# First attention of a two-part transformer kernel: key maximum added by the tensor engine, copies and small steps moved between engines

## The chip, the cores and the metric

The kernel runs on one core of one Trainium2 chip. The metric is device time in microseconds (us). A core has five engines that run at the same time, each with its own queue of instructions in order: PE (matrix multiplies; its weight loads are listed as PEld), DVE (vector work), ACT (activation functions and copies), POOL (general vector work, in SBUF only) and SP, which issues the DMAs. Matmul results stand in PSUM, eight banks of 512 f32 columns for 128 partitions; everything else stands in SBUF.

## The reference, cut to what matters

Sixteen sequences of 256 positions with 128 channels pass through a first windowed attention, then through six layers of attention and feed-forward. The change touches the first attention only:

```
x = x + first(layernorm(x))
# first: 64 windows of 64 positions, 16 heads of 8 channels
qkv = (xw @ W_qkv).reshape(B * nw, 64, 3, 16, 8)
q = layernorm(q, ln_gamma, ln_beta)      # over the 8 channels of a head
k = layernorm(k, ln_gamma, ln_beta)
attn = softmax(einsum('bqhd,bkhd->bhqk', q * SCALE, k))   # SCALE = 1
out = einsum('bhqk,bkhd->bqhd', attn, v).reshape(B * nw, 64, 128)
out = out @ W_proj + b_proj
...
x = x + six_layers(layernorm(x))         # attention + feed-forward, not touched
```

## The kernel before

**The two parts.** `first_attention` (lines 297 to 547) runs first, in PSUM pools and SBUF pools of its own. When its pools are given back, the main loop (from line 906) runs 192 tiles of the six layers; there the order of PE is pinned by hand. In the first attention it is not: the compiler is called with a scheduling option (line 1015) and orders each engine's instructions from its own estimates of their times, so the order on an engine is not that of the program text. What each engine gets is in order from then on: an instruction that waits holds all that stand behind it in its queue.

**Units and stages.** The first attention works on eight units of two sequences: four token tiles (t) of 128 positions, each of which holds two windows (c). The outer loop has 25 steps k; in each, `merge` interleaves pieces of six stages that belong to different units, so that several units are in flight:

- `stage_load`: `row_stats` gets the mean and the sum of squares of each row (lines 319 to 323) on ACT, the weight of the values `rv` on DVE (370); PE transposes the tile, ACT and DVE write it as two halves, `xnt`; POOL adds the projection's bias to `xt` (378), for later.
- `stage_qkv`: three matmuls per token tile into a bank `pq` (387); ACT and DVE write q and k (388) and the values as fp16 high and low halves (392, 393). Then, for all 32 heads of q and k, squares (ACT, 397), their sums (DVE, 399), `rsqrt` on 128 columns (DVE and ACT in turn, 307 to 313), the scaling (DVE, 401), gamma and beta (POOL, 402 and 403).
- `stage_heads`: q (s = 0) and k (s = 1) are written as fp16 halves with four places per head: the high half by ACT (414), the low half by POOL (415), and the second copies of both by DVE (417, 419). A transposing DMA on SP's queue turns them (421).
- `stage_soft`: sixteen small matmuls fill one bank `ps` (439; two banks, `bufs` 2), DVE takes the maximum over keys (448) and subtracts it on the way to SBUF (449). When a token tile is whole, ACT takes the exponential (459) and writes the high half (461), POOL the low half (462), and a transposing DMA turns both (464).
- `stage_out`: per window half c, 24 matmuls with the values into a bank `po` (480), DVE takes the reciprocal of the sums (482) and multiplies (485); then a PE transpose (493), an ACT copy (495), the projection (500) and the sum with x (DVE, 507).
- `stage_norm`: the result goes out by DMA (513), `row_stats` again, scaled rows on ACT (518), PE transposes (522) and two ACT copies into `xg` (524, 525), from which the main loop starts.

**Weights.** From step 6 on the first layer's weights are loaded and prepared in between (`first_weights`), which takes some ACT, DVE and PE time.

**PSUM.** `SPLIT0` (line 34) gives the banks of the first attention: two for `pq`, two for `ps`, two for `po`, one for `py`, one for `pt`.

Of the kernel before, what the change touches and what calls it, by code (L numbers as in the profile page):

```python
# [12 lines left out]
HP = mybir.dt.float16  # L13
# [20 lines left out]
SPLIT0 = (2, 2, 2, 1, 1)  # L34
# [21 lines left out]
def kernel(  # L56
# [30 lines left out]
    make_identity(nc, ident)  # L87
    onesm = const.tile([128, 128], F32, name="onesm")
# [208 lines left out]
    def first_attention(p1, p2, p3, pqp, psp0, pop, pyp, ptp=None):  # L297
        ptp = ptp or pyp
        def rsqrt(dst, src, scale):
            if dst.shape[1] != 128:  # L300
                S.activation(dst, src, AF.Ln, bias=epst, scale=scale)
                S.activation(dst, dst, AF.Exp, scale=-0.5)
                return
            n = dst.shape[1]
            a = p3.tile([128, n], F32, name=f"rqa{n}")
            b = p3.tile([128, n], F32, name=f"rqb{n}")
            V.tensor_scalar(b, src, scale, EPS, ALU.mult, ALU.add)
            S.activation(a, b, AF.Ln)
            S.activation(a, a, AF.Exp, scale=-0.5)
            V.tensor_tensor(b, b, a, ALU.mult)  # L310
            V.tensor_tensor(b, b, a, ALU.mult)
            V.tensor_scalar(b, b, -0.5, 1.5, ALU.mult, ALU.add)
            V.tensor_tensor(dst, b, a, ALU.mult)

        def row_stats(xt, pre):
            mu = p3.tile([128, 4], F32, name=f"{pre}mu")
            rs = p3.tile([128, 4], F32, name=f"{pre}rs")
            sq = p3.tile([128, 128], F32, name="sq0")
            for t in range(4):
                S.activation(sq, xt[:, t], AF.Copy, scale=-1.0 / 128.0, accum_out=mu[:, t : t + 1])  # L320
            for t in range(4):
                S.activation(sq, xt[:, t], AF.Square, bias=mu[:, t : t + 1], accum_out=rs[:, t : t + 1])
            rsqrt(rs, rs, 1.0 / 128.0)
            return mu, rs
# [22 lines left out]
        dma(bpt, bp0.partition_broadcast(128))  # L347
        pm = pqp.tile([128, 512], F32, name="pq")
# [15 lines left out]
        def stage_load(u):  # L364
            if u:
                load_x(u)
            e = U[u]
            _, e.rs = row_stats(e.xt, "a")
            e.rv = p1.tile([128, 4], F32, name="rv")
            V.tensor_scalar(e.rv, e.rs, VPRE, None, ALU.mult)  # L370
            yield
            e.xnt = p1.tile([128, 2, 4, 128], FR, name="xnt")
            pt = ptp.tile([128, 4, 128], F32, name="pt" if ptp is not pyp else "py")
            for t in range(4):
                T.transpose(pt[:, t], e.xt[:, t], ident)
            S.copy(e.xnt[:, 0], pt)
            V.tensor_tensor(e.xnt[:, 1], pt, e.xnt[:, 0].bitcast(F32), ALU.subtract)
            G.tensor_tensor(e.xt, e.xt, bpt.unsqueeze(1).to_broadcast([128, 4, 128]), ALU.add)
            yield
# [26 lines left out]
        def stage_heads(u):  # L406
            e = U[u]
            e.hl = []
            for s in range(2):
                src = e.qk[:, :, s * 128 : s * 128 + 128].rearrange("p t (h d) -> p t h d", d=8)  # L410
                hl = p1.tile([128, 4, 16, 4, 8], HP, name=f"hl{s}")
                for t in range(4):
                    hi, lo = hl[:, t, :, 0], hl[:, t, :, 2 if s else 1]
                    S.copy(hi, src[:, t])
                    G.tensor_tensor(lo, src[:, t], hi, ALU.subtract)
                    if s:
                        V.tensor_copy(hl[:, t, :, 1:4:2], hl[:, t, :, 0:3:2])
                    else:
                        V.tensor_copy(hl[:, t, :, 2:4], hl[:, t, :, 0:2])
# [7 lines left out]
        def stage_soft(u, n2):  # L427
            e = U[u]
            p0 = p2.tile([128, 2, 8, 128], F32, name="p0")
            for n in range(2):  # L430
                t = 2 * n2 + n
                for jj in range(2):
                    ps = psp0.tile([128, 4, 2, 64], F32, name="ps")
                    for i in range(4):
                        for c in range(2):
                            cols = slice(64 * c, 64 * c + 64)
                            for vp in range(2):
# [5 lines left out]
                                    start=True,  # L443
                                    stop=True,
                                )
                    nm = p2.tile([128, 8], F32, name="nm0", bufs=4)
                    psf = ps.rearrange("p i c k -> p (i c) k")
                    V.tensor_reduce(nm, psf, AX.X, ALU.max)
                    V.tensor_tensor(
                        p0[:, n, 4 * jj : 4 * jj + 4].rearrange("p i (c k) -> p (i c) k", c=2),  # L450
                        psf,
                        nm.unsqueeze(2).to_broadcast([128, 8, 64]),
                        ALU.subtract,
# [3 lines left out]
            for n in range(2):  # L457
                pf = p0[:, n]
                S.activation(pf, pf, AF.Exp)
                ph = p2.tile([128, 2, 8, 128], HP, name="ph")  # L460
                S.copy(ph[:, 0], pf)
# [5 lines left out]
        def stage_out(u, n2):  # L467
            e = U[u]
            for n in range(2):
# [3 lines left out]
                o0 = p3.tile([128, 2, 8, 8], F32, name="o0")  # L473
                for c in range(2):
                    r = slice(64 * c, 64 * c + 64)
                    po = pop.tile([128, 8, 18], F32, name="po")
                    for gm in range(8):
                        p = gm % 4 * 2 + gm // 4
                        for q, (a, b) in enumerate(((0, 0), (0, 1), (1, 0))):
                            T.matmul(po[:, p], pt0[r, a * 8 + gm], v[r, b, p], start=(q == 0), stop=(q == 2))  # L480
                    rc = p3.tile([128, 8], F32, name="rc0")
                    V.reciprocal(rc, po[:, :, 16])
                    for hp in range(2):
                        h = slice(64 * hp, 64 * hp + 64)
                        V.tensor_tensor(
                            o0[h, c],
                            po[h, :, hp * 8 : hp * 8 + 8],
                            rc[h].unsqueeze(2).to_broadcast([64, 8, 8]),
                            ALU.mult,
                        )  # L490
# [76 lines left out]
    identh = keep.tile([128, 128], HP, name="identh")  # L567
    V.tensor_copy(identh, ident)
# [451 lines left out]
```

## Time and profile before

| | us |
|---|---|
| median of 3 runs (lowest, highest) | 3285.94 (3284.38, 3286.59) |
| profiled execution, its own time | 3280.49 |
| its span, first to last instruction | 3278.7 |
| granted PE clock, mean | 0.996 |

The span cut into stretches, busy us of each engine:

| stretch, us | PE | DVE | ACT | POOL |
|---|---|---|---|---|
| 0 to 50 | 19.39 | 31.66 | 34.22 | 21.41 |
| 260 to 290 | 22.26 | 20.28 | 19.56 | 20.01 |
| 290 to 3278 | 2851.68 | 2359.46 | 2176.59 | 2347.06 |

The first stretch is the start of the first attention; its first score matmul (L439) begins near 52 us, its last one ends near 254.7. In 260 to 290 the last units leave while the main loop begins: its first matmul starts at 269.72, and the last copy into `xg` ends at 286.7. From there on the main loop runs alone.

How to read it: busy time is the time an engine had an instruction in work. The duration of a matmul includes the time to pass through the array, so matmuls in a row overlap and cost less than the mean of one. A row of the groups gives line, engine, operation, output and inputs, shapes, count, then busy us and mean ns of one, then the idle time of the engine just before such instructions, with what ended it.

### The profile page before, as it was taken

Reading aid. Unit: us, or ns where it says so; the run is one execution under the profiler, and the core shown is the slowest. Engines: PE = TensorE matmul, PEld = TensorE weight load, DVE = VectorE, ACT = ScalarE, POOL = GpSimd, SP = SyncE. Lnnn points to the kernel's source line nnn. Section 1 sums busy time; section 2 is a strip of 40 time slices with the busy share of each in tenths; the row PEclk is TensorE's granted clock in tenths of the full one; section 3 lists DMA queues with packets and bytes.
Section 4 is the critical chain, followed back from the end, with each engine's and each line's share of the span. In section 5 each row is a group of like instructions: output and inputs, shape, how many; then the busy total and the mean of one; then the engine's idle time right before and its main releaser. Section 6 shows DMA issues by size and latency. Waiting matters only on the chain. (4 is left out here: it accounts for less than half of the span.)

```text
span 3278.7 us, 159366 instructions
## 1 busy us (share of the span) xinstructions
PE 3062.1 (93%) x70178; PEld 2157.8 (66%) x70178; DVE 2596.0 (79%) x4850; ACT 2388.8 (73%) x5034; POOL 2511.2 (77%) x2578
## 2 busy tenths in 40 slices
PE   4887999999999999999999999999999999999996
PEld 3665666666666666666666666666666666666664
DVE  7987788887788887788787788887788887777773
ACT  6876777777777777777777777777777777766773
POOL 5657888877888877888877888878888778777771
PEclk9999999999999999999999999999999999999998
DMA  4763444344354343454343344444454443434442
GB/s 110 132 130 77 99 101 102 83 88 91 82 104 99 83 90 88 83 107 95 84 92 85 86 108 92 85 95 82 89 104 91 91 90 81 91 89 90 86 88 56
DMA packets 622969, 303.31 MB, mean 93 GB/s; under 512 B 533446, under 2 KB 545732, under 8 KB 622276
## 3 DMA queue, kind: packets, MB, share of 16 engines
q1 hardware_dynamic: 622276, 293.11, 42.7%
q8 instruction: 552, 9.04, 1.1%
q14 instruction: 141, 1.16, 0.1%
HBM read 22.38 MB, written 4.19 MB: 8 GB/s over the span
## 5 line engine op out<-in xcount | busy, mean ns | idle before, releaser
L291 PE MATMUL bank<-wqkv,xhl 128*128 128x512 f16 x3456 | 1238.3, 380 | 7.9 <-ACT sq L651 7.6
L653 POOL TENSOR_TENSOR sum<-mc 128x512 f32<-128x512 f32 x768 | 993.9, 1297 | 285.7 <-DVE mc L642 275.0
L642 DVE TENSOR_TENSOR mc<-bank,tq 128x1024 f32<-128x1024 f32 x768 | 929.8, 1220 | 186.1 <-PE bank L294 178.3
L663 POOL TENSOR_TENSOR sum<-sum,r 128x512 f32<-128x512 f32 x768 | 797.6, 1059 | 31.9
L652 DVE TENSOR_REDUCE r<-sq 128x8 f32<-128x512 f32 x768 | 519.8, 682 | 283.2 <-ACT sq L651 276.0
L294 PE MATMUL bank<-ident,sum 128*128 128x128 f32 x3072 | 712.9, 273 | 24.2 <-DVE of L796 24.2
L801 POOL TENSOR_TENSOR ohl<-of,ohl 128x512 f16<-128x512 f32 x384 | 451.3, 1175 | 226.0 <-ACT ohl L800 225.3
L651 ACT ACTIVATE sq<-bank 128x512 f32<-128x512 f32 x768 | 458.7, 608 | 150.6 <-DVE mc L642 148.3
L294 PEld LDWEIGHTS bank<-ident,sum 128*128 128x128 f32 x3072 | 432.4, 141 | 182.2 <-issue 67.6
L291 PEld LDWEIGHTS <-xhl 128*128 128x128 f16 x3456 | 340.0, 98 | 181.8 <-issue 17.9
L800 ACT CAST ohl<-of 128x512 f16<-128x512 f32 x384 | 237.8, 619 | 283.9 <-DVE of L796 278.9
L291 PE MATMUL bank<-vb,pt 64*32 64x65 f32 x6144 | 384.5, 225 | 31.6 <-ACT pt L620 21.0
L291 PEld LDWEIGHTS bank<-vb,pt 64*32 64x32 f32 x6144 | 263.0, 105 | 191.5 <-ACT p L275 49.0
L294 PE MATMUL bank<-ident,p 128*128 128x128 f32 x1536 | 354.8, 273 | 0.9 <-issue 0.9
L291 PEld LDWEIGHTS bank<-kt,qt 64*32 64x32 f32 x27648 | 289.1, 105 | 91.6 <-issue 91.6
L291 PE MATMUL bank<-v,pt 64*32 64x65 f32 x6144 | 319.5, 225 | 30.1 <-ACT gt L281 13.4
L291 PE MATMUL bank<-vw,pt 64*32 64x65 f32 x12288 | 336.5, 225 | 0.0
L291 PE MATMUL bank<-kt,qt 64*32 64x64 f32 (+1 forms) x27648 | 312.9, 216 | 9.5 <-issue 9.5
L291 PE MATMUL bank<-ot,wohl 128*128 128x128 f16 x4608 | 294.8, 221 | 4.6 <-DMA ot<-ohl 4.6
L796 DVE TENSOR_TENSOR of<-bank,rc 128x256 f32<-128x256 f32 x768 | 292.4, 416 | 1.6
L620 ACT COPY kt<-bank 128x512 f32<-128x512 f32 x384 | 226.3, 589 | 70.9 <-PE bank L294 65.1
L291 PEld LDWEIGHTS <-wohl 128*128 128x128 f16 x4608 | 261.8, 99 | 22.7 <-DMA ot<-ohl 4.8
(155 smaller groups left out, 5130.5 us busy)
## 6 DMA issues: line engine op xcount, KB each, us to landing
v<-vb SPq DMA_DIRECT2D x384, 130.0 KB
vw<-vb SPq DMA_DIRECT2D x384, 130.0 KB
vw<-vb SPq DMA_DIRECT2D x576, 65.0 KB
wraw<-in_L_ffn_Wqkv_dram SPq DMA_DIRECT2D x36, 256.0 KB
wraw<-in_L_ffn_Wo_dram SPq DMA_DIRECT2D x12, 256.0 KB
ot<-ohl SPq DMA_TRANSPOSE x192
xt<-in_L_attn_x_dram SPq DMA_DIRECT2D x8, 256.0 KB
r1d<-xt SPq DMA_DIRECT2D x8, 256.0 KB
```

What stands on the lines that cost most here:

```text
L291: pin(T.matmul(*args, **how))
L294: pin(T.transpose(*args))
L620: S.copy(to[:, mb * 4 : mb * 4 + 4], hold[0])
L642: V.tensor_tensor(prod, p4.unsqueeze(3).to_broadcast([128, 8, 2, 2, 32]), tq[:, s, d.j].unsqueeze(1).to_broadcast([128, 8, 2, 2, 32]), ALU ...
L651: S.activation(sq, pp.rearrange("p (h d) -> p h d", d=64), AF.Square)
L652: V.tensor_reduce(r[:, hb * 8 : hb * 8 + 8], sq, AX.X, ALU.add)
L653: G.tensor_tensor(mc, m2[:, :, 0], m2[:, :, 1], ALU.add)
L663: G.tensor_tensor(mc, mc, rb.unsqueeze(2).to_broadcast([128, 8, 64]), ALU.mult)
L796: V.tensor_tensor(of[:, :, a], po[a][:, :, 0:64], rc.unsqueeze(2).to_broadcast([128, 4, 64]), ALU.mult)
L800: S.copy(ohl[:, 0, h], of)
L801: G.tensor_tensor(ohl[:, 1, h], of, ohl[:, 0, h], ALU.subtract)
```

## The change

It has six parts, all in the first attention. (1) The score matmuls leave their group open; the negated maximum is written as fp16, and PE adds it to the bank by a matmul of an fp16 identity with the maximum broadcast over 64 keys; ACT takes the exponential straight from PSUM, per half tile, with a factor SDIV = 16. For that gamma and beta are multiplied once by SDIV to the power -0.5, and the fp16 identity is made at the start instead of before the main loop. (2) ACT and POOL write both copies of the halves of q and k themselves, from an input read twice; the DVE copies go. (3) The high half of the probabilities is cast by DVE instead of ACT. (4) Both window halves of the values' product stand in one tile of two banks, so that reciprocal and multiplications are done once for both; the pool has one such tile instead of two single banks. (5) The row sums come from one DVE reduction and a POOL scaling instead of four ACT copies that accumulate. (6) The vector steps of the 128-column `rsqrt` and `rv` run on POOL instead of DVE.

```diff
-SPLIT0 = (2, 2, 2, 1, 1)
+SPLIT0 = (2, 2, 1, 1, 1)
...
+    identh = const.tile([128, 128], HP, name="identh")
+    V.tensor_copy(identh, ident)
...
-            V.tensor_scalar(b, src, scale, EPS, ALU.mult, ALU.add)
+            G.tensor_scalar(b, src, scale, EPS, ALU.mult, ALU.add)
             S.activation(a, b, AF.Ln)
             S.activation(a, a, AF.Exp, scale=-0.5)
-            V.tensor_tensor(b, b, a, ALU.mult)
-            V.tensor_tensor(b, b, a, ALU.mult)
-            V.tensor_scalar(b, b, -0.5, 1.5, ALU.mult, ALU.add)
-            V.tensor_tensor(dst, b, a, ALU.mult)
+            G.tensor_tensor(b, b, a, ALU.mult)
+            G.tensor_tensor(b, b, a, ALU.mult)
+            G.tensor_scalar(b, b, -0.5, 1.5, ALU.mult, ALU.add)
+            G.tensor_tensor(dst, b, a, ALU.mult)
...
-            for t in range(4):
-                S.activation(sq, xt[:, t], AF.Copy, scale=-1.0 / 128.0, accum_out=mu[:, t : t + 1])
+            V.tensor_reduce(mu, xt, AX.X, ALU.add)
+            G.tensor_scalar(mu, mu, -1.0 / 128.0, None, ALU.mult)
...
+        for g in (gam, bet):
+            G.tensor_scalar(g, g, SDIV**-0.5, None, ALU.mult)
...
-            V.tensor_scalar(e.rv, e.rs, VPRE, None, ALU.mult)
+            G.tensor_scalar(e.rv, e.rs, VPRE, None, ALU.mult)
...
+                hi, lo = (slice(0, 2), slice(2, 4)) if s else (slice(0, 3, 2), slice(1, 4, 2))
                 for t in range(4):
-                    hi, lo = hl[:, t, :, 0], hl[:, t, :, 2 if s else 1]
-                    S.copy(hi, src[:, t])
-                    G.tensor_tensor(lo, src[:, t], hi, ALU.subtract)
-                    if s:
-                        V.tensor_copy(hl[:, t, :, 1:4:2], hl[:, t, :, 0:3:2])
-                    else:
-                        V.tensor_copy(hl[:, t, :, 2:4], hl[:, t, :, 0:2])
+                    two = src[:, t].unsqueeze(2).to_broadcast([128, 16, 2, 8])
+                    S.copy(hl[:, t, :, hi], two)
+                    G.tensor_tensor(hl[:, t, :, lo], two, hl[:, t, :, hi], ALU.subtract)
...
-                                    start=True,
-                                    stop=True,
+                                    start=(i == 0 and c == 0),
+                                    stop=False,
+                                    skip_group_check=True,
                                 )
-                    nm = p2.tile([128, 8], F32, name="nm0", bufs=4)
+                    nm = p2.tile([128, 8], HP, name="nm0", bufs=4)
                     psf = ps.rearrange("p i c k -> p (i c) k")
-                    V.tensor_reduce(nm, psf, AX.X, ALU.max)
-                    V.tensor_tensor(
+                    V.tensor_reduce(nm, psf, AX.X, ALU.max, negate=True)
+                    T.matmul(
+                        psf,
+                        identh,
+                        nm.unsqueeze(2).to_broadcast([128, 8, 64]),
+                        start=False,
+                        stop=True,
+                        skip_group_check=True,
+                    )
+                    S.activation(
                         p0[:, n, 4 * jj : 4 * jj + 4].rearrange("p i (c k) -> p (i c) k", c=2),
                         psf,
-                        nm.unsqueeze(2).to_broadcast([128, 8, 64]),
-                        ALU.subtract,
+                        AF.Exp,
+                        scale=SDIV,
                     )
...
-                S.activation(pf, pf, AF.Exp)
                 ph = p2.tile([128, 2, 8, 128], HP, name="ph")
-                S.copy(ph[:, 0], pf)
+                V.tensor_copy(ph[:, 0], pf)
                 G.tensor_tensor(ph[:, 1], pf, ph[:, 0], ALU.subtract)
...
+                both = pop.tile([128, 2, 512], F32, name="po")
+                po = both[:, :, 0:144].rearrange("p c (m e) -> p c m e", e=18)
                 for c in range(2):
                     r = slice(64 * c, 64 * c + 64)
-                    po = pop.tile([128, 8, 18], F32, name="po")
                     for gm in range(8):
                         p = gm % 4 * 2 + gm // 4
                         for q, (a, b) in enumerate(((0, 0), (0, 1), (1, 0))):
-                            T.matmul(po[:, p], pt0[r, a * 8 + gm], v[r, b, p], start=(q == 0), stop=(q == 2))
-                    rc = p3.tile([128, 8], F32, name="rc0")
-                    V.reciprocal(rc, po[:, :, 16])
-                    for hp in range(2):
-                        h = slice(64 * hp, 64 * hp + 64)
-                        V.tensor_tensor(
-                            o0[h, c],
-                            po[h, :, hp * 8 : hp * 8 + 8],
-                            rc[h].unsqueeze(2).to_broadcast([64, 8, 8]),
-                            ALU.mult,
-                        )
+                            T.matmul(po[:, c, p], pt0[r, a * 8 + gm], v[r, b, p], start=(q == 0), stop=(q == 2))
+                rc = p3.tile([128, 2, 8], F32, name="rc0")
+                V.reciprocal(rc, po[:, :, :, 16])
+                for hp in range(2):
+                    h = slice(64 * hp, 64 * hp + 64)
+                    V.tensor_tensor(
+                        o0[h],
+                        po[h, :, :, hp * 8 : hp * 8 + 8],
+                        rc[h].unsqueeze(3).to_broadcast([64, 2, 8, 8]),
+                        ALU.mult,
+                    )
...
-    identh = keep.tile([128, 128], HP, name="identh")
-    V.tensor_copy(identh, ident)
```

## The prediction

> **What bounds the kernel now.** I first cut the span into stretches, since the change touches only the first attention, which ends before 290 us. Columns of this view: stretch, its length, busy us and instructions of PE, PEld (weight loads), DVE, ACT and POOL, the granted clock, the DMA share, GB/s.
>
> ```profile
> 0.00:50.00 50.00, 19.39 (x54) 13.48 (x55) 31.66 (x61) 34.22 (x132) 21.41 (x62) 1.00 0.37 104
> 50.00:260.00 210.00, 168.74 (x2842) 127.35 (x2841) 184.56 (x475) 158.41 (x442) 122.67 (x102) 1.00 0.68 128
> ```
>
> In the middle 210 us DVE is busy 184.6 (88%), PE 168.7 (80%), ACT 158.4 (75%), POOL 122.7 (58%), DMA 68%. Then the groups of instructions of the first 300 us, which hold what the change edits: count, busy us, mean ns, idle time before and who ended it.
>
> ```profile
> L462 POOL TENSOR_TENSOR ph<-p,ph 128x1024 f16<-128x1024 f32 x32 | 71.1, 2223 | 72.3 <-ACT ph L461 68.1 <-DVE nm L448 4.2
> ...
> L448 DVE TENSOR_REDUCE nm<-ps 128x8 f32<-128x512 f32 x64 | 43.8, 684 | 2.8 <-PE ps L439 2.0
> L449 DVE TENSOR_TENSOR p<-ps,nm 128x512 f32<-128x512 f32 x64 | 43.4, 680 | 1.2
> ...
> L459 ACT ACTIVATE p<-p 128x1024 f32<-128x1024 f32 x32 | 33.7, 1052 | 21.8 <-DVE p L449 21.7
> L461 ACT CAST ph<-p 128x1024 f16<-128x1024 f32 x32 | 33.3, 1040 | 6.6 <-DMA pt<-ph 6.2
> ...
> L485 DVE TENSOR_TENSOR o<-po,rc 64x64 f32<-64x64 f32 x128 | 28.0, 218 | 1.9
> L415 POOL TENSOR_TENSOR hl<-qk,hl 128x128 f16<-128x128 f32 x64 | 25.1, 429 | 2.5 <-ACT hl L414 2.5
> ...
> L417 DVE COPY hl<-hl 128x256 f16<-128x256 f16 x32 | 15.1, 488 | 0.2
> ...
> L419 DVE COPY hl<-hl 128x256 f16<-128x256 f16 x32 | 13.2, 444 | 5.7 <-POOL hl L415 5.6
> ```
>
> The reader sees DVE rows with hardly any idle time, so they are never waiting, while others wait for them. The list of waits in 50 to 260 says the same: POOL's wait for ACT is the end of a chain that begins with ACT's wait for the DVE subtraction, and PE's score matmuls wait for that subtraction to free their bank.
>
> ```profile
> POOL ph L462 <- ACT ph L461: 64.0, 17, 7.8
> ACT p L459 <- DVE p L449: 21.7, 16, 3.7
> ...
> PEld L439 <- DVE p L449: 17.6, 14, 2.9
> PE po L480 <- DMA pt<-ph: 15.2, 11, 2.9
> ...
> PE ps L439 <- DVE p L449: 13.7, 11, 2.8
> ```
>
> So DVE bounds the middle. Last I looked at DVE and POOL side by side, for what happens when both read SBUF:
>
> ```profile
> 124.14 2.36 POOL L402 TENSOR_TENSOR qk<-qk,gam 128x1024 f32<-128x1024 f32 x1
> ...
> 268.51 1.00 POOL L580 MEMSET vw<- 128x520 f32 x2
> ```
>
> ```profile
> 125.01 1.52 DVE L370 TENSOR_SCALAR rv<-ars 128x4 f32<-128x4 f32 x1
> ...
> 268.95 0.65 DVE L568 CAST identh<-ident 128x128 f16<-128x128 f32 x1
> ```
>
> L370 works on 4 columns and elsewhere takes 0.16; here it lasts 1.52 and ends with POOL's L402 (126.50). The f32 to f16 cast lasts until POOL's memsets are over. Such DVE instructions wait out a running POOL instruction; the reverse shows at 149.50, where L462 takes 3.10 instead of 2.12 beside the DVE's L401.
>
> **The change, part by part.** Durations are means of rows of the first 300 us unless another place is named.
>
> DVE loses 64 subtractions (43.4), the hl copies (15.1 + 13.2 = 28.3), five steps of rsqrt (L307 4.6, L310 3.3, L311 4.1, L312 1.8, L313 3.6: 17.4) and L370 (4.0). The output steps become 32 reciprocals (0.21, so 6.7 for 12.7) and 64 multiplications of 64x128 (L822, the nearest row, 0.285: 18.2 for 28.0): 15.8 less. It gains 16 reductions of the row sums (L652, 512 elements from SBUF, 0.682: 10.9) and 32 casts of 1024 elements. No row has such a cast. One-source rows of 128 (L312, 0.219) and 384 (L224, 0.360) elements give 0.55 ns an element, so 0.71; at the plain rate of the 1024-element reduction L399 it would be 1.21. I take 0.71, since L357, a cast of 384 in 0.352, lies on the fast line: 22.7. Net -75.5 us. The cast can also wait behind a POOL instruction, from nothing up to a whole L462 (2.13): up to 68 us more, the upper end.
>
> ACT loses 64 accumulating copies L320 with their reads (19.4 + 12.2 = 31.6) and the cast L461 (33.3). Its 32 exponentials of 1.052 become 64 from PSUM (L275 with p<-bank, 0.618: 39.6 for 33.7, +5.9) and its 64 hl casts write both copies (L594, 128x256, 0.411 for 0.294: +7.5). Net -51.5.
>
> POOL gains: L415 at double size (L595, a subtraction of 256 elements, 0.668 for 0.429: +15.3; at most twice 0.429, +27.5), per unit three products of 128 elements (0.429) and two scalings (0.27, between L659's 0.244 and the 0.292 of the select on ident), for eight units 14.6, and 24 tiny ones of at most 0.244: 5.9. Together +36, of which 29 fall in the middle: 122.7 becomes 152. The two scalings of gam and bet (0.5) are done before anything needs them. These steps also queue on POOL: the mean's scaling waits for a DVE reduction and holds up L402, L403, L415 and L462 behind it, and the rsqrt steps wait twice (for ACT's Exp). ACT's squares wait for the mean; for the second normalisation that is under 0.7 + 0.24 plus one POOL instruction of 2.35, hidden because the main loop starts on earlier sequences (269 us, while the last unit ends at 286.7). Uncovered, it would be 3 us once.
>
> PE gains 64 matmuls of 512 columns of the form L291 bank<-nm,identh (0.379 each). Where two run back to back the second costs 0.21 (two of L291 at 288.00 take 0.59). So 13.4 to 24.3; I take 13.8. In the middle PE goes from 168.7 to 182.5, or 193.
>
> Now the new wait: score matmuls, DVE reduction (0.684, f16 output L743 0.686), the new PE matmul, ACT exponential, then the bank is free. That is two hops more on PE's own queue, and behind a matmul that waits stand the PV, projection and qkv matmuls, for whose results DVE, ACT and the DMA transposes wait. The compiler orders PE by estimated times, and the timeline of before has 16 score matmuls split by PV work, so other work can stand in the gap. Each of the two banks turns once in 6.3 us (64 tiles in 202 us); the new chain is 0.64 + 0.68 + 0.38 + 0.62 and four hops of about 0.1, 2.7 us, so bank supply hides it. One po tile of two banks costs 0.2 + 2 x 0.285 = 0.8 of DVE before PE may refill it; a token tile comes each 6.3 us, so that is hidden; without cover 32 x 0.8 = 26.
>
> What is late next? DVE falls in the middle to about 118 and ACT to 118. Left are PE with 182.5 and what DVE and POOL share: 152 of POOL, 31 casts (22) and six L401 (7), 181 us. Neither is far under today's 184.6, so most of the DVE gain does not pass through. What passes: DVE reached 88% as a bound; with two slack engines beside it I take 90% for the shared pair, 181/0.9 = 201, so 210 - 201 = 9, rounded to 10 since PE alone gives 182.5/0.9 = 203 and its dense cost is lower than its busy time.
>
> Start: ACT is full from 10 to 30 us; about eight L320 pairs (0.43 apart, 3.4 us) stand before the first unit's L397, and the DVE copies end 2.4 after POOL (48.9 against 46.5). Against that stand doubled subtractions (two sides, 1.1 each) and the slower rsqrt (0.4): -3. End: from the last score matmul (254.6) to the last subtraction L462 (264.0) pass 9.4 us; the new chain of 0.68 + 0.38 + 0.62 + 0.71 + 2.12 with hops is 5; queues take some, so -3.
>
> Sum -10 - 3 - 3 = -16. Nothing after 290 us changes but its start. The profiled execution took 3280.49 (span 3278.7 and 1.8 around it), so 3264.5; the median of the runs is 5.45 higher, 3285.94, which gives **3270**.
>
> The Trainium skill ("SBUF — State Buffer", section "SBUF: two separate sides") says that a Vector instruction in a two-port mode and a GpSimd instruction exclude each other for the whole instruction, which speaks against moving the cast to DVE and the small steps to POOL. The L370 and L568 rows agree with it; if it holds for every pair, the sum is the 181 above with every cast in line, and if it did not hold, POOL's 152 would bound nothing and PE's 203 would stand.
>
> **The rivals.**
>
> A, large gain: DVE was the only hard bound and PE's busy time is soft. PE's rows overstate. Run together in the timeline, 16 score matmuls take 0.57, 48 of L480 1.30, three of L387 1.20, eight of L500 1.06, one of L493 0.36, four of L375 or L522 1.05; 64 x 0.57 + 32 x (1.30 + 1.20 + 1.06 + 0.36) + 16 x 1.05 = 179 for the stage, against 190 busy (19.4 + 168.7 + 9 after 260, less 7.5 of weight set-up). The middle is then 168.7 x 179/190 + 13.8 = 173; at 95% 182, -28, with start and end -34: 3252. For it speaks that DVE now ends most waits; against it the shared pair's 181.
>
> B, no change: the wait returns on PE. If half of reduction and matmul (0.684 + 0.379) is uncovered at each tile, 64 x 0.53 = 34 us of idle PE take the place of the 31 us that PE now waits for L449 (17.6 + 13.7, if the two rows do not overlap): +3, and with start and end -3: 3283. Against it the mixed order in PE's queue.
>
> C, slower: the shared pair, at the cast in front of L462. If each cast waits for a POOL instruction while its own L462 cannot start, and each of 31 hand-overs leaves the pair idle for 0.5, 181 + 16 = 197, at 90% 219: +9, with start and end eaten by the same queues: 3295. It decides once the casts last over 1.2 us on average, half a POOL instruction of waiting.
>
> **How the numbers follow.** Forecast (-7 to -26) 0.46, A 0.20, B 0.17, C 0.17. Under 0.2% (6.6 us) a measurement of this kernel cannot be told from no change. Faster 0.66, same 0.17, slower 0.17. The range goes from 3249, a little under A (its 182 at 3 us less), to just short of C, 3294.
>
> **What would show it.** Right: DVE under 70% busy in the middle, POOL over 70%, the first score matmuls 2 to 5 us earlier than 52.6, the main loop's first matmul (269.7) some 16 earlier, all later stretches of equal length. C: casts of 1.2 us and more that end with POOL instructions. B: PE idle for the DVE reduction ahead of the new matmul. Wrong altogether: a change in the length of what follows 290 us, where I expect none.

## The result, and the profile after

| | before | after |
|---|---|---|
| median, us | 3285.16 (6 runs, 3280.13 to 3286.59) | 3303.77 (6 runs, 3298.64 to 3309.55) |
| profiled execution, its span | 3280.49, 3278.7 | 3303.46, 3301.7 |
| first score matmul, last score matmul's end | 52.6, 254.6 | 47.8, 267.2 |
| main loop's first matmul | 269.7 | 281.1 |

The change made the kernel slower by 18.6 us: a ratio of 1.006, interval 1.0047 to 1.0073. The forecast was 3270, with a range up to 3294. In the profiles the start became 4.8 us shorter, the stretch with score matmuls 17.4 longer (202.0 to 219.4), what is between it and the main loop 1.2 shorter: 11.4 in all. The rest, about 7, is in the main loop.

The stretches of after, with the columns of the first view of the prediction:

```profile
0.00:50.00 50.00, 21.52 (x94) 16.35 (x95) 28.07 (x48) 31.22 (x94) 30.46 (x80) 0.68 0.41 115
50.00:260.00 210.00, 185.24 (x2710) 124.95 (x2711) 133.11 (x256) 119.53 (x343) 152.45 (x145) 0.52 0.65 119
260.00:290.00 30.00, 23.57 (x317) 14.36 (x308) 18.34 (x39) 12.59 (x35) 14.57 (x17) 0.60 0.41 84
```

DVE lost 51 us in the middle and is busy for 63% of it; POOL's 152.45 is the 152 of the prediction. Both are now far from full, and PE is not: 185.24, 88%. The granted clock there is 0.52. The page of before had shown full clock for the same stretch. Groups of after in its first 300 us:

```profile
L471 POOL TENSOR_TENSOR ph<-p,ph 128x1024 f16<-128x1024 f32 x32 | 69.7, 2179 | 38.5 <-DVE ph L470 34.6 <-issue 3.5
...
L450 DVE TENSOR_REDUCE nm<-ps 128x8 f16<-128x512 f32 x64 | 42.7, 683 | 4.2 <-PE ps L440 3.3
L451 PE MATMUL ps<-nm,identh 128*128 128x512 f16 x64 | 38.2, 606 | 7.2 <-DVE nm L450 6.9
L459 ACT ACTIVATE p<-ps 128x512 f32<-128x512 f32 x64 | 37.4, 592 | 38.1 <-PE ps L451 37.3 <-PE ps L440 0.5
...
L470 DVE CAST ph<-p 128x1024 f16<-128x1024 f32 x32 | 29.5, 921 | 14.7 <-ACT p L459 6.7 <-DMA pt<-ph 3.5 <-issue 2.8
```

The new matmul (L451) lasts 0.606 where the prediction's row had 0.379. The waits of after, 50 to 260:

```profile
ACT p L459 <- PE ps L451: 33.9, 28, 2.8
POOL ph L471 <- DVE ph L470: 30.9, 12, 7.4
...
DVE xt L517 <- PE py L510: 23.9, 18, 3.5
...
DVE rc L492 <- PE po L490: 20.2, 17, 2.8
ACT v L396 <- PE po L490: 17.4, 9, 2.7
...
PE ps L451 <- DVE nm L450: 6.9, 7, 1.6
```

Before, DVE ended the waits of PE and ACT. Now PE ends those of ACT and DVE, at four different lines: PE is what is late.

### The profile page after: what moved, and what is told of

The parts are those of the page before. It is cut to its first block, busy times and chain, and to the rows that moved or that the text cites. A ratio compares the mean times of both kernels' runs of the same rounds, so it can differ in the third digit from the quotient of the medians.

```text
span 3301.7 us, 159235 instructions
## 1 busy us (share of the span) xinstructions
PE 3097.8 (94%) x70242; PEld 2169.4 (66%) x70242; DVE 2547.7 (77%) x4626; ACT 2350.6 (71%) x4906; POOL 2554.6 (77%) x2644
## 5 line engine op out<-in xcount | busy, mean ns | idle before, releaser
L296 PE MATMUL bank<-ident,sum 128*128 128x128 f32 x3072 | 713.8, 274 | 26.2 <-DVE of L804 24.4
L293 PE MATMUL bank<-vb,pt 64*32 64x65 f32 x6144 | 387.2, 225 | 31.1 <-ACT pt L628 20.2
L293 PEld LDWEIGHTS bank<-vb,pt 64*32 64x32 f32 x6144 | 263.0, 105 | 190.5 <-ACT p L277 49.0
L293 PE MATMUL bank<-v,pt 64*32 64x65 f32 x6144 | 320.8, 225 | 31.0 <-ACT gt L283 13.4
L293 PEld LDWEIGHTS <-wohl 128*128 128x128 f16 x4608 | 263.3, 99 | 24.3 <-DMA ot<-ohl 4.7
```

Of the source, the lines that this page charges most:

```text
L293: pin(T.matmul(*args, **how))
L296: pin(T.transpose(*args))
```

## The clock of the first attention

The prediction priced the new matmul at 0.21 us when it stands in a row with others, from two L291 at 288.00. The granted clock is drawn from records of its changes. The trace of before holds none ahead of 274.2 us, so its page shows full clock where nothing is known (the first line below, in tenths of full speed over 40 slices of the span), while that of after has its first at 14.2 (the second):

```profile
PEclk9999999999999999999999999999999999999998
```

```profile
PEclk6557999999999999999999999999999999999998
```

The matmuls told it all the same. This is the beginning of the main loop in the timeline of before (start, us, engine, line):

```profile
269.72 2.74 PE L291 MATMUL bank<-wqkv,xhl 128*128 128x512 f16 x6
...
276.88 0.81 PE L291 MATMUL bank<-wqkv,xhl 128*128 128x512 f16 x3 [1.07 <-ACT sq L651]
```

Six matmuls of one form start 0.43 us apart, and seven us later three of the same form 0.215 apart. The record at 274.2 stands between them.

To see the price in the first attention, each PE matmul is charged with the time up to the next one's start, at most its own duration; what is left is idle. Between the first and the last score matmul this gives, in us:

| kernel | stretch | occupied | of it added matmuls (each) | idle |
|---|---|---|---|---|
| before | 201.8 | 164.2 | - | 37.6 |
| after | 219.2 | 193.0 | 32.5 (0.525) | 26.2 |
| undo_max | 198.1 | 157.8 | - | 40.3 |
| only_max | 221.6 | 189.2 | 30.1 (0.485) | 32.4 |
| narrow | 206.7 | 170.5 | 10.5 (0.170) | 36.2 |
| no_wait | 203.8 | 184.6 | 26.3 (0.418) | 19.2 |
| pad128 | 211.9 | 162.5 | - | 49.4 |
| only_max_pad128 | 217.9 | 188.7 | 31.3 (0.504) | 29.2 |

So the added matmuls occupy PE for 32.5 us instead of 13.8, and all the relief of DVE, ACT and the queues took 11.4 off PE's idle time.

The Trainium skill ("TensorE: Matmul & The Clock Gate", section "Wait — 56ns, not 53.3ns?") gives 426.7 ns from start to start for 512 columns while the array is at half clock, and 215.7 at full clock; the 0.43 and 0.215 above agree. The 0.485 to 0.525 of the table lie above its first figure, and the 0.418 of no_wait, at a mean clock of 0.66, lies just under it. Its section "What's actually happening" has full clock granted after one busy window of about 3.4 us; here PE was busy for 80 to 88% of 210 us, and their mean granted clock was 0.50 (one_layer_before, below) and 0.52 (after).

**one_layer_before, one_layer_after.** Both kernels with one of the six layers.

```diff
-LAYERS = 6
+LAYERS = 1
```

> The kernel before with one of the six layers (five left out), so that the first attention is a larger share and a drift in the long main loop cannot enter; to be set against one_layer_after. If the first attention alone makes the whole loss of 18.6, the two differ by 18 to 20; if it makes the 11.4 of the profiles and the rest is the main loop's, by 10 to 13.

> The changed kernel with one of six layers (five left out). First attention alone makes the loss: 18 to 20 us over one_layer_before; 11.4 from it and the rest from the long main loop: 10 to 13 us.

Measured 833.24 and 845.92, a difference of 12.7, as the 11.4 of the profiles asked for; main loops start at 269.2 and 280.0. The first attention makes 11 of the 18.6, the rest needs the long main loop. This trace of the first attention of before holds clock records:

```profile
50.00:260.00 210.00, 168.97 (x2844) 127.60 (x2842) 184.64 (x476) 158.63 (x443) 122.70 (x101) 0.50 0.69 128
```

Its busy times are those of before to 0.3 us, at clock 0.50. The first attention ran at half clock before the change, too.

## Experiments on the first attention

**undo_max, only_max.** Part 1 taken out of the change; part 1 put alone into before.

```diff
-                    V.tensor_reduce(nm, psf, AX.X, ALU.max, negate=True)
-                    T.matmul(
+                    V.tensor_reduce(nm, psf, AX.X, ALU.max)
+                    V.tensor_tensor(
...
-                        AF.Exp,
-                        scale=SDIV,
+                        nm.unsqueeze(2).to_broadcast([128, 8, 64]),
+                        ALU.subtract,
...
+                S.activation(pf, pf, AF.Exp)
```

> The changed kernel with the maximum subtracted by DVE again, exponential from SBUF, everything else as changed. P: PE has 34 us less work, DVE 43 more (176 of 210 in the middle, what it had before or less), main loop from 255 to 266, earlier than the 269.7 of before. Q: 272 to 284, later than before. Length from the main loop's first matmul to the end: 3009 if the longer main loop of the changed kernel (3020.6) comes with the added matmuls, 3020 if with something else.

> The kernel before with the maximum added by PE and nothing else of the change. P: PE 34 us more, main loop from 274 to 290, later than before (269.7). Q and a pure DVE bound: 245 to 262, since DVE loses 43 us. Length of the main loop: 3020 if it comes with the added matmuls, 3009 if not.

undo_max: 3281.83, ratio 0.9985 (0.9975 to 0.9994), main loop from 261.4, as P had it. only_max: 3307.51, ratio 1.0068 (1.0053 to 1.0083), main loop from 290.5, just past the 290 that P gave at most. Part 1 costs 19.7 within the change and 20.8 alone; the other five parts together gain 8.3. Their middles:

```profile
50.00:260.00 210.00, 165.08 (x2875) 125.44 (x2874) 181.40 (x343) 125.84 (x337) 160.19 (x149) 0.51 0.70 129
```

```profile
50.00:260.00 210.00, 177.82 (x2605) 121.67 (x2607) 148.35 (x381) 151.33 (x446) 115.49 (x100) 0.57 0.62 118
```

undo_max (first) has DVE at 86% and PE at 79% and is 20 us ahead of after; only_max (second) has DVE at 71% and its main loop starts last of the four. A relieved DVE is not the point here.

**narrow.** After, but the new matmul adds to 64 of the 512 columns.

```diff
-                        psf,
+                        psf[:, :, 0:8],
                         identh,
-                        nm.unsqueeze(2).to_broadcast([128, 8, 64]),
+                        nm.unsqueeze(2).to_broadcast([128, 8, 8]),
...
-                        scale=SDIV,
+                        scale=1.0,
```

> The changed kernel, but the new matmul adds the maximum to 8 of each 64 keys only (64 columns instead of 512; the exponential's factor is 1 instead of 16, so that nothing overflows); all waits stay. Theory P (PE is the bound, because in this stage the new matmul takes PE 0.53 us and not 0.21): 64 x 0.4 = 26 us less PE work, and the main loop's first matmul comes at 255 to 266 instead of 281.1. Theory W (the new wait of PE for the DVE reduction, not the matmul's length): 277 to 284. Theory Q (DVE and POOL shutting each other out at the casts and the small steps): 277 to 284.

3290.67, ratio 1.0017 (1.0007 to 1.0026); main loop from 271.4, between the two expectations. Its row, for L451 of after at 606:

```profile
L451 PE MATMUL ps<-nm,identh 128*128 128x64 f16 x64 | 14.8, 235 | 3.8 <-DVE nm L450 3.8
```

22 us of PE's work went and 10 us of idle time came (36.2 for 26.2): without its length part 1 costs 10.0 instead of 19.7 (271.4 and 281.1 against 261.4).

**twice, four_dense.** After with a second such matmul behind the first, and after with four ahead of each half tile's score matmuls, both of zeros.

```diff
+                    for z in range(4):
+                        T.matmul(
+                            ps.rearrange("p i c k -> p (i c) k"),
+                            identh,
+                            zeroh.unsqueeze(2).to_broadcast([128, 8, 64]),
+                            start=(z == 0),
+                            stop=False,
+                            skip_group_check=True,
+                        )
...
-                                    start=(i == 0 and c == 0),
+                                    start=False,
```

> The changed kernel with a second matmul of 512 columns that adds zeros to each score tile, behind the first; no new wait. P: 64 x 0.43 to 0.53 = 28 to 34 us more PE work, main loop from 305 to 317 instead of 281.1. W: 279 to 287. Q: 279 to 287.

> The changed kernel with four matmuls of 512 columns that add zeros at the head of each score tile (no wait but for the bank). The trace after shows PE at half clock in the first attention (0.52) and at 1.00 in the main loop, whose matmuls are large. H (the clock follows how dense PE's work is): the granted clock of 50 to 260 rises over 0.8, all PE work there halves in length, and the main loop begins before 281. P without H: 64 x 4 x 0.29 (the step of the doubled matmul) = 74 us more, 345 to 365.

twice: 3315.95, ratio 1.0092 (1.0077 to 1.0107), main loop from 299.5, between P's 305 and the others' 287: 18.4 later for 64 matmuls, 0.29 each. four_dense: 3310.6, ratio 1.0074 (1.0061 to 1.0088), main loop from 295.0: 256 matmuls for 14 us. Its middle:

```profile
50.00:260.00 210.00, 195.27 (x2800) 116.51 (x2800) 131.83 (x250) 120.28 (x347) 152.51 (x145) 0.87 0.70 119
```

The clock rose to 0.87, as H had it. The faster clock carried most of the added work, but the main loop did not start before 281, which H had too.

**no_wait.** After with zeros in place of the maximum, and the reduction behind the matmul, so that PE waits for nobody (the maximum is computed and left out).

```diff
-                    V.tensor_reduce(nm, psf, AX.X, ALU.max, negate=True)
                     T.matmul(
                         psf,
                         identh,
-                        nm.unsqueeze(2).to_broadcast([128, 8, 64]),
+                        zeroh.unsqueeze(2).to_broadcast([128, 8, 64]),
...
+                    V.tensor_reduce(nm, psf, AX.X, ALU.max, negate=True)
...
-                        scale=SDIV,
+                        scale=1.0,
```

> The changed kernel, but the new matmul adds zeros (its length stays 512 columns) and the DVE reduction stands behind it, so PE never waits for DVE there; the maximum is left out and the exponential's factor is 1. P (matmul length on a full PE): 278 to 283 for the main loop's first matmul, as 281.1 before this edit. W (the wait between scores and matmul makes the half of the loss that the narrow matmul left: 271.4 against 261.4 without the matmul): 268 to 274.

3291.32, ratio 1.0015 (1.0006 to 1.0024); main loop from 265.5, earlier than either theory had. Its middle:

```profile
50.00:260.00 210.00, 189.24 (x2934) 133.27 (x2930) 149.96 (x278) 123.48 (x364) 158.13 (x149) 0.66 0.71 127
```

By the table the stretch is 15.4 shorter than in after: idle 7.0 less, the new matmul 6.2 less (0.418 for 0.525, at a clock of 0.66 for 0.52), the rest 2.2 less. So the wait on PE's queue was not hidden, though the prediction had it so; the row of after named 6.9 of it. Against undo_max, part 1 costs 4.1 without the wait (265.5 for 261.4) and 10.0 without the length (narrow). The two gains, 15.6 and 9.7, are together more than the 19.7 of part 1, and taking the wait away also raised the clock, so how much of the loss is wait and how much is length stays open.

**q_undone.** After with the cast on ACT (part 3 undone) and the small steps on DVE (part 6, and the mean's scaling of part 5).

```diff
-            G.tensor_tensor(b, b, a, ALU.mult)
+            V.tensor_tensor(b, b, a, ALU.mult)
...
-                V.tensor_copy(ph[:, 0], pf)
+                S.copy(ph[:, 0], pf)
```

> The kernel after with the cast of the probabilities' high half back on ACT (part 3 undone) and the small steps of rsqrt, of the row mean's scaling and of rv back on DVE (part 6 and half of 5 undone); PE's added matmul stays. P (PE and its wait for the reduction bound): DVE and POOL part, but PE's work stays, so the main loop starts at 277 to 284 as in after. Q (the pair of DVE and POOL that share SBUF bounds): casts cost DVE nothing and POOL loses some 20 us, so the main loop starts under 275.

3309.67, ratio 1.0074 (1.006 to 1.0087); main loop from 284.1, at the end of P's range.

```profile
50.00:260.00 210.00, 184.50 (x2716) 125.69 (x2715) 122.10 (x271) 147.03 (x378) 129.67 (x101) 0.55 0.64 119
```

POOL is 23 us lower, DVE 11, and nothing came of it: what DVE and POOL share is not what bounds here. PE's 184.5 stayed, and the stretch with score matmuls, 216.5 us for 219.4, has PE idle for 26.1 us as in after (26.2); it began 3.5 later.

**halves.** After, with the maximum of every second half tile added by DVE on the way to SBUF, so 32 matmuls instead of 64.

```diff
+                    if jj:
+                        V.tensor_tensor(pj, psf, nm.unsqueeze(2).to_broadcast([128, 8, 64]), ALU.add)
+                        S.activation(pj, pj, AF.Exp, scale=SDIV)
+                    else:
```

> The kernel after, but only the first half tile of each pair has the maximum added by PE; in the second, DVE adds the fp16 maximum on the way to SBUF and ACT takes the exponential there. P (each added matmul has a price of its own, step plus chain): 32 of the 64 matmuls are gone, so the main loop starts half way between the 261.4 of undo_max and the 281.1 of after, 267 to 276, and PE spends 15 to 18 us on the matmuls left. Q (DVE is a bound too): sharing the work between PE and DVE beats both, the main loop starts under 261. R (one matmul per pair costs as much as two, since the chain is what counts): 277 to 284.

Main loop from 270.0, in P's range, with 15.4 us of PE's time in the 31 matmuls counted. Yet the total was 3320.72, ratio 1.0107 (1.0093 to 1.012): the main loop took 3046. That led to the runs further below.

**undo1_cast_act, two_parts.** undo_max with the cast on ACT as before; and before with parts 2 and 4 alone.

```diff
-                V.tensor_copy(ph[:, 0], pf)
+                S.copy(ph[:, 0], pf)
```

> The kernel after with the maximum subtracted by DVE again (part 1 undone) and the cast of the probabilities' high half on ACT again (part 3 undone); the other four parts stay. P (PE's steps at half clock bound the first attention, and what is left beside them is PE waiting for DVE's subtraction): DVE loses 29.5 us of casts, which beside POOL last 0.92 us each, so PE's 40.3 us of idle time among the scores shrink and the main loop starts at 250 to 260, ahead of the 261.4 of undo_max; total under 3281.8. S (DVE is not what PE waits for there): the main loop starts at 261 or later, total 3282 or more.

> The kernel before with parts 2 and 4 alone: ACT and POOL write both copies of the halves of q and k, and both window halves of the values' product stand in one tile; the fp16 identity is made at the start. P (PE waits for DVE): DVE loses 28 us of copies and 16 us of output steps, PE nothing gains, so the main loop starts at 250 to 262, total 3268 to 3283. S (what DVE loses is not on the path): 266 to 272, total 3283 to 3289.

undo1_cast_act: 3276.29, ratio 0.9974 (0.9965 to 0.9983), though its main loop starts at 261.2, as in undo_max, which is the start that S gave: by this run PE did not wait for those casts, and the gain over undo_max is not in the first attention. two_parts: 3273.01, ratio 0.9959 (0.9946 to 0.9971), main loop from 257.1, as P had it. It is the fastest kernel with all six layers, 12.7 under the before of its comparison and 30.8 under after.

```profile
50.00:260.00 210.00, 175.43 (x2967) 131.20 (x2967) 161.71 (x345) 168.49 (x462) 141.69 (x113) 0.52 0.70 131
```

Its stretch with score matmuls is 190.5 us long for 202.0, so later work falls into this window, and PE's 175 is above the 169 of before. Between the scores PE has no more work than before (160.4 us occupied for 164.2) and waits 7.6 us less (30.0 for 37.6).

## Experiments on the main loop and on the order

The main loop has the same order of PE's matmuls in all kernels, but for swaps of neighbours in the records. Its length, the median less its start and the 1.8 around the span, is 3013.7 in before, 3020.9 in after and 3049 in halves. It does not simply come with the added matmuls, which undo_max and only_max were also to show: in their profiles it is 3021.6 without them and 3016.2 with them, for 3009.0 in before and 3020.6 in after. In halves, all but one of PE's gaps of over 0.6 us stand 2816 PE instructions apart, or multiples of that, if the instructions of PE's sequencer (waits for semaphores above all) are counted with the matmuls and weight loads. The table of DMA queues in the page of before (packets, MB, share) has a queue of its own for code:

```profile
q8 instruction: 552, 9.04, 1.1%
```

9.04 MB in 552 packets is 16.4 KB each, and PE's 140,356 matmuls and weight loads and 1018 sequencer instructions, together over 552, make 256. Four tiles of the main loop are 2816 instructions, 11 x 256. So the idea (F): code comes in blocks of 256 instructions, the edges of the blocks fall in the same places of every fourth tile, and the count of PE instructions ahead of the main loop sets which. Six kernels shift that count by matmuls of zeros at the start, 32 in pad64, 64 in pad128, 128 in pad256 on before, 96 on halves, 64 on after and on only_max:

```diff
         T.matmul(pm[:, 0:384], onesm, w0r, start=True, stop=True)
+        zh = const.tile([128, 8], HP, name="zh")
+        G.memset(zh, 0.0)
+        for _ in range(32):
+            T.matmul(pm[0:8, 448:456], zh, zh, start=True, stop=True)
```

> The kernel before with 32 more matmuls of 8 columns of zeros at its very start (64 PE instructions with their weight loads), into columns of a bank that nothing reads; nothing else changes. F (PE's code is fetched in blocks of 256 instructions, and where the blocks' edges fall in the main loop sets how often PE waits for code; four tiles of the main loop are 2816 instructions, 11 blocks, so the edges fall in the same places throughout): the count of PE instructions ahead of the main loop is that of halves modulo 256, so the main loop takes 3038 to 3055 as there, PE's gaps put down to issue there grow to 30 us and more, and the total is 3308 to 3325. W (halves' long main loop has another cause): the main loop stays at 3009 to 3019, total 3283 to 3293.

> The kernel before with 64 more matmuls of 8 columns of zeros at its very start (128 PE instructions with their weight loads), into columns that nothing reads; nothing else changes. F (edges of code blocks): the count ahead of the main loop is that of after modulo 256, so the main loop takes 3016 to 3025 instead of 3009 to 3015, and the total is 4 to 12 above before. W (what lengthens the main loop of after has another cause): main loop 3009 to 3015, total within 4 of before, since the matmuls at the start cost at most 4.

> halves with 96 more matmuls of 8 columns of zeros at its very start (192 PE instructions with their weight loads), into columns that nothing reads. F (edges of code blocks): the count ahead of the main loop is that of before modulo 256, so the main loop falls from 3046 to 3009 to 3019 while the first attention keeps its 270 (up to 276 with the added matmuls): total 3283 to 3296 for 3320.7. W: the main loop stays over 3040, total 3315 or more.

> The kernel after with 64 more matmuls of 8 columns of zeros at its very start (128 PE instructions with their weight loads), into columns that nothing reads. F (edges of code blocks): the count ahead of the main loop is that of before modulo 256, so the main loop takes 3009 to 3016 instead of 3021 and the total is 3294 to 3302, though the added matmuls may cost up to 4 at the start. W: the main loop stays at 3018 to 3024, total 3302 or more.

> only_max (the kernel before with part 1 alone) with the 64 matmuls of zeros of pad128 at its start, which also change the order that the compiler deals in the first attention. Pad128 without part 1 has its main loop start at 278.2. P (part 1 costs what it costs whatever the order): the main loop starts at 294 to 303, 16 to 25 after that of pad128. R (before's order is an unusually good one and part 1 mostly spoils it): 279 to 288, at most 10 after that of pad128. F (edges of code blocks; the count ahead of the main loop is that of before modulo 256): main loop 3009 to 3016.

> The kernel before with 128 matmuls of 8 columns of zeros at its very start (256 PE instructions with their weight loads), into columns that nothing reads. F (edges of code blocks): the count ahead of the main loop is that of before modulo 256 again, so the main loop takes 3009 to 3016, though it has more added instructions than pad64 with its 3093. W (the added matmuls themselves lengthen the main loop): over 3025. R (the order dealt by the compiler, which here stays nearer to that of before than in pad64 and pad128, sets the start): the main loop starts at 270 to 275, before the 278 of pad128 though it has twice the zeros; otherwise at 278 or later.

| kernel | median | ratio (interval) | main loop from | its length (profile) |
|---|---|---|---|---|
| pad64 | 3367.87 | 1.0244 (1.0229 to 1.026) | 282.1 | 3093.0 |
| pad128 | 3297.62 | 1.0034 (1.0021 to 1.0046) | 278.2 | 3016.8 |
| pad256 | 3291.94 | 1.0013 (1.0002 to 1.0023) | 273.8 | 3016.0 |
| halves_pad192 | 3294.7 | 1.0024 (1.0015 to 1.0034) | 273.1 | 3019.8 |
| after_pad128 | 3300.03 | 1.0039 (1.0026 to 1.0051) | 280.0 | 3023.7 |
| only_max_pad128 | 3307.43 | 1.0052 (1.0036 to 1.0069) | 284.7 | 3021.5 |

**Code blocks.** 32 matmuls that nobody reads made the main loop of before longer by 84 us, more than F had; 128 of them by 7, by the medians 3; 96 took 26 off that of halves. PE's waits in pad64 from 300 on, and one of them in the timeline:

```profile
PE bank L291 <- issue: 60.6, 44, 2.4
```

```profile
387.87 1.69 PE L291 MATMUL bank<-kt,qt 64*32 64x64 f32 x155
391.55 0.28 PE L291 MATMUL bank<-kt,qt 64*32 64x32 f32 x5 [1.99 <-issue]
```

Of the 35 gaps over 0.6 us between 330 and 2850 us in pad64, 34 stand at one and the same place, the 194th, of a block of 256 recorded PE instructions, in halves 29 of 30. The stretch of the same 56,500 main-loop matmuls, and PE's idle time at those places (192 to 195) from 60 to 2600 us of the loop:

| matmuls and weight loads ahead of the loop, modulo 256 | kernels | stretch, us | idle at the edges |
|---|---|---|---|
| 139 | before | 2472.4 | 0.1 |
| 139 | eight others | 2471.6 to 2479.5, mean with before 2474.2 | 1.8 to 5.4 |
| 11 | after | 2481.4 | 8.6 |
| 11 | six others | 2477.5 to 2483.1, mean with after 2480.3 | 3.7 to 6.9 |
| 203 | halves | 2513.0 | 36.8 |
| 203 | pad64 | 2556.8 | 61.6 |

After's main loop is 9.0 longer than that of before in this stretch, and its idle time at the edges 8.5 more. The two agree. But the zeros that were to bring the loop of after back to the place of before did not shorten it: after_pad128 came to 2479.5 and its profile's main loop to 3023.7, where F gave 3016 at most, and only_max_pad128, at 2475.7 in this stretch, to 3021.5.

The count that F used leaves something out. The sequencer's instructions take places in the blocks too: without them the gaps of pad64 stand 2795 to 2797 apart, with them 2816 as in halves. And the kernels hold different numbers of them ahead of the loop, 41 in before and 56 in after_pad128. Counted with them, the loop begins at place 180 of a block in before, pad256 and two_parts and 181 in undo1_cast_act, and these four stretches agree within 1 us (2471.6 to 2472.5). At 185 to 193 they are 2473.0 to 2475.8 (four kernels), at 195, in after_pad128, 2479.5, at 48 to 66 (the seven of the rows with 11) 2477.5 to 2483.1, at 240 (pad64) 2556.8, at 255 (halves) 2513.0. So after_pad128 was not back at the place of before, and no kernel with the order of after was run there. What differs outside this stretch stays open: the profiled main loop of two_parts is 3016.7 us long and that of before 3009.0, with the same place and nearly the same stretch.

The Trainium skill ("Runtime: NRT & Kernel Launch", section "Instruction fetch mechanics") has code refilled in blocks of 256 instructions, as the packets and the places of the gaps show; it calls the cost of a block's edge mostly hidden. In before it was, in pad64 it was 62 us.

**The order.** pad128's first attention is 8.5 us longer and pad64's 12.4, while pad256, with 128 matmuls of zeros, is 4.1 longer, in the range that R gave. The compiler dealt pad64 and pad128 another order, nearly the same in both, though their starts lie 3.9 apart. Of PE's first 2000 matmuls in the trace, the zeros left out, 57% have in pad64 and in pad128 the tiles and shape that stand at the same place in before; in pad256 it is 99.6%. Between the scores PE has no more to do in pad128 (162.5 us for 164.2), but it is idle for 49.4 us instead of 37.6. A part of that is a longer wait for the subtraction, in 50 to 260 of pad128 beside the 13.7 of before:

```profile
PE ps L443 <- DVE p L453: 17.5, 11, 2.8
```

On pad128's order part 1 costs 6.5 us (only_max_pad128, 284.7 for 278.2), which is R's case and not P's. Its matmuls take 31.3 there as elsewhere, but the idle time that it removes is 20.2 instead of 5.2. So 14 of the 20.8 us of only_max hang on the order. The order is another one in nearly every kernel here (leaving the added matmuls out, after has at 51% of the first 2000 places what before has), so each start above carries an uncertainty of that kind, up to about 12 us in one start. Two things stand clear of it. The added matmuls occupy PE for 30 to 33 us in after, in q_undone (30.1) and on both orders of only_max. And of the kernels with parts 2 and 4, the three with all 64 matmuls, full length and wait and no further matmuls among the scores (after, after_pad128, q_undone) start the main loop at 280.0 to 284.1, the three without the added matmuls (undo_max, undo1_cast_act, two_parts) at 257.1 to 261.4.

## Why the prediction was wrong, point by point

- **The step that failed: "Where two run back to back the second costs 0.21 ... So 13.4 to 24.3; I take 13.8."** The row was from the main loop at full clock; in the first attention a step took 0.525 at half clock, and the 64 matmuls occupied PE for 32.5 us, beyond even the upper end. With 64 x 0.525 = 33.6 the prediction's own rule gives (168.7 + 33.6)/0.9 = 225 for the middle, +15; measured were +17.4. That this comes so near is partly luck: the order alone made the stretch 10 to 12 longer in pad128 and pad64.
- **What bounds.** "Left are PE with 182.5 and what DVE and POOL share" was weighed the wrong way round. PE, with its work and its waits, is what is late; q_undone took 23 us from POOL and 11 from DVE for nothing.
- **"so bank supply hides it"** put the new wait at nothing. Its chain was compared with a bank's turn, not with PE's queue. Without the wait (no_wait) the main loop starts 15.6 earlier: 7.0 of idle time, and shorter steps at a higher clock.
- **"Nothing after 290 us changes but its start."** The main loop grew by 7.2 by the medians. In the profiles its measured stretch is 9.0 longer, with 8.5 more idle time at the edges of code blocks, which the 128 added PE instructions moved; no run has shown after's loop short again at the place of before, so this cause fits but is not shown. The prediction had named a change there as its sign of being wrong altogether.
- **Right.** DVE under 70% (63%), POOL over 70% (73%, 152.45 for 152), first score matmuls 4.8 earlier (2 to 5), the po tile and the small POOL steps without visible cost. The end gave 1.2 instead of 3. DVE's 133 in the middle was to be 118; the casts are 6 of the difference: 22 of the 32 took 0.63 to 0.73, as priced, and ten took longer.
- **The rivals.** A fell with PE. B had the right side of the matter, a wait on PE for the reduction, but at 34 us; the row shows 6.9. C gave the nearest time (3295) for a reason that did not happen: casts averaged 0.921, under its 1.2. Single ones did wait, as here in the timeline of after:

```profile
151.81 2.36 POOL L407 TENSOR_TENSOR qk<-qk,bet 128x1024 f32<-128x1024 f32 x1
151.85 2.88 DVE L470 CAST ph<-p 128x1024 f16<-128x1024 f32 x1
```

## What to carry to other kernels

Price an added matmul by a row from the same stretch, and look at the start-to-start times of one form for the clock, since a clock curve without records in a stretch says nothing about it. Moving work from an engine at 88% to one at 80% pays only if the second engine's price is known to well under the difference: here the gainful parts (2 and 4) were those that gave PE nothing. Before a few microseconds are ascribed to an edit, test with an edit that does no work: it can move the order that the compiler deals (up to 12 us here) and the edges of the code blocks (70 in pad64, by the medians, for 32 matmuls of zeros).

## What the runs showed of the hardware that was not expected

- PE, busy for 80 to 88% of 210 us with mostly small matmuls, had a mean granted clock of 0.50 (one_layer_before) and 0.52 (after); with four more long matmuls per half tile the mean rose to 0.87 (four_dense).
- The place of a code block's edge in a loop cost PE up to 2.4 us at a time and 62 us in pad64, 0.1 in before, with the same matmuls in the same order. The instructions of PE's sequencer count for that place.
